# Layer 1's feed-forward: seven block products of sums in place of eight, a pair of batches at a time

## The chip, the cores and the metric

The kernel runs on one core of a Trainium2 chip. A core has five engines that run at the same time and meet at semaphores: TensorE (PE, matrix products; it loads a 128x128 operand, the weights, and streams the other through it), VectorE (DVE), ScalarE (ACT), GpSimd (POOL) and SyncE (SP, which here only issues DMAs). Each engine executes its own instructions in a fixed order. Operands lie in SBUF, 128 partitions wide; products land in PSUM, eight banks of 128 x 512 f32, which DVE and ACT can read and POOL can't. The metric is the time of one execution on the device in microseconds (us).

## The reference

Two layers, each with a cross attention and a feed-forward, over 4 batches of 512 tokens with 512 numbers each. The change touches the feed-forward of the last layer:

```python
up_gate = jnp.einsum('bsd,hd->bsh', x, W1)        # W1, W3: (2048, 512)
up_lin = jnp.einsum('bsd,hd->bsh', x, W3)
hidden = jax.nn.silu(up_gate) * up_lin
hidden = fwht(hidden)                             # Walsh-Hadamard over the 2048
out = jnp.einsum('bsh,dh->bsd', hidden, W2)       # W2: (512, 2048)
...
x = x + jnp.tanh(g_ffn[1]) * _L1_ffn_ref(_layernorm(x, axis=-1), ...)
```

## The kernel before

The order of the run is layer 0 (its attention and feed-forward), layer 1's attention, layer 1's feed-forward. Only the last part, and the pieces that are prepared for it during the attention, are touched.

*Number format.* PE takes f32 operands as they are for transposes, and a rounded form of them (fp32r) for most products. To keep the precision, an operand is split into a high part (rounded copy, made by ACT) and a low part (operand minus high, made by DVE from PSUM with `split`, by POOL from SBUF with `split_sb`). A product then takes three matmuls (`three`): high times low, low times high, high times high.

*Layer 1's feed-forward before* (L1391 to L1459). The 2048 hidden numbers are 16 tiles `f` of 128. For each tile the weights are prepared once (`prepare`): the rows of W1, W3 and of W2 (already partly transformed over the hidden index, from device memory) are loaded, transposed on PE against the identity into PSUM (`pw`), and split; W2's also go through a product with the 128x128 Hadamard matrix (`had`): transposes `pw`, a split into `hs`, the product `ph`, a split into `w2T`. The transforms of the hidden vector are so moved into W2. The normalised tokens of a batch are kept transposed and split (`xg`, by `normalise`).

The loop goes over pairs of tiles `n` (8 of them), in each over the 4 batches `b`, in each over the two tiles. Per tile and batch there is a product with W1 and one with W3: 4 chunks of the 512 input numbers x 3 matmuls, each 128x128 against 128x512, into a PSUM bank `p`. ACT takes the silu of the first (L1443), DVE multiplies by the second (L1444), `split_sb` makes high and low part `gg` on ACT and POOL (L125, L126), and `down` adds the product with W2 to four accumulators `acc` (L1419). After two tiles DVE adds the scaled `acc` to the residual `x` (L1454). In the last pair the result goes out by DMA.

*What sets the order.* The program is written in the order of the text, and the builder then orders each engine's instructions by its own simulated timeline. Where the text says `tc.manual_schedule(engines={nc.tensor.engine})`, PE keeps the order of the text. Before, that holds for layer 1's attention and not for the feed-forward. Side work (weights to prepare, tokens to normalise) is kept in a list `jobs` of generators; each call of `work()` takes the next steps up to a `yield`. A tile in SBUF or PSUM is reused by its tag in rotation (`bufs` of them), and its next writer waits for its last reader. All DMAs are issued by SP, in one order.

Of the kernel before, what the change touches and what calls it, by code (L numbers as in the profile page):

```python
# [21 lines left out]
P = 128  # L22
NB = 4
# [19 lines left out]
def flamingo_kernel(  # L43
# [52 lines left out]
    one_d = scratch("one_d", [2, S])  # L96

# [941 lines left out]
    with ExitStack() as l1:  # L1039
# [18 lines left out]
        def prepare(f, sp, bank, hp, htag, staged=None):  # L1058

            weights[f] = []
            fetched = []
            if staged is None:
                fetched.extend(fetch(f, i, sp) for i in range(2))
                yield
                yield
            pool, tag = (qz, f"qw{f % 2}") if f % 4 < 2 else (fi, f"w13_{f % 2}")
            w13 = pool.tile([P, 2, 2, ND, P], FR, tag=tag, name=f"w13T_{f}")  # L1070
            pairs = [w13[:, 0], w13[:, 1]]

            def kept(i, shape):
                wt = pairs[i] if i < 2 else w2_tile(f, f"w2T_{f}")
                weights[f].append((wt[:, 0], wt[:, 1]))
                return weights[f][-1]

            for i in range(3):
                st = fetched[i] if staged is None else staged[i]
                pt = bank([P, ND, P], f"pw{i}_{f}")  # L1080
                for k in range(ND):
                    nc.tensor.transpose(pt[:, k, :], st[:, k, :], ident)  # L1082
                if staged is None and i == 0:
                    fetched.append(fetch(f, 2, sp))
                if i < 2:
                    split(*kept(i, [ND, P]), pt)
                    yield
                    if staged is None and i:
                        yield
                        yield  # L1090
                        yield
            pt = pt.rearrange("p c q -> p (c q)")
            hs = [hp.tile([P, D], FR, tag=htag, name=f"hs{i}_{f}") for i in range(2)]
            split(*hs, pt)
            yield
            if staged is None:
                yield
            ph = bank([P, D], f"ph2_{f}")
            products(ph, [(had, hs[1]), (had, hs[0])])
            split(*kept(2, [D]), ph, 1.0 / math.sqrt(F))  # L1100
            yield

        xgT = [None] * NB

        def normalise(b, xg, xn_pool, bank, xn_tag="xn", ahead=False):

            xgT[b] = (xg[:, 0], xg[:, 1])
            return layernorm_split(b, f"g{b}", xg, xn_pool, bank, xn_tag, ahead)


        with ExitStack() as at:
# [216 lines left out]
            with tc.manual_schedule(engines={nc.tensor.engine}):  # L1328
                for s in range(-3, 4 * last + 2):
# [3 lines left out]
                    if s in (24, 40):  # L1333
                        jobs.append(prepare(s // 20 - 1, ap_, side, xnp, "xn"))
# [39 lines left out]
                    if s == 55:  # L1374
                        jobs.append(normalise(0, stack_tile(2, "xg0"), xnp, side, ahead=True))
                    if s > 20 and s % 16 == 6:
                        jobs.append(finish(n // NO - 1))
                    if s == 60:
                        jobs.append(normalise(1, stack_tile(0, "xg1"), xnp, side, ahead=True))
                    if s == 63:  # L1380
                        jobs.append(normalise(2, stack_tile(1, "xg2"), xnp, side, ahead=True))
# [9 lines left out]
        with ExitStack() as l2:  # L1391
            fi = pool_in(l2, "fi")
            fs = pool_in(l2, "fs", 3)
            gp = pool_in(l2, "gp1", 2)
            ps = pool_in(l2, "ps1", 3, space=PSUM)
            ps_acc = pool_in(l2, "ps_acc1", space=PSUM)
            side = banks_of(pool_in(l2, "ps_m1", 1, space=PSUM))

            def fetched(f):
                staged = [fetch(f, i, fs, 3) for i in range(3)]  # L1400
                jobs.append(prepare(f, fs, side, fs, "hs", staged))

            for n in range(NF // 2):
                for b in range(NB):
                    if n == 0 and b == 2:
                        xg3 = qz.tile([P, 2, ND, S], FR, tag="xn3", name="xg3")
                        jobs.append(normalise(3, xg3, fs, lambda shape, name: ps.tile(shape, F32, tag="h", name=name)))
                    if b < 2 and n + 1 < NF // 2:
                        fetched(2 * n + 2 + b)
                    acc = [  # L1410
                        ps_acc.tile([P, D], F32, tag=f"acc{t}", name=f"acc1_{n}_{b}_{t}")
                        for t in range(NT)
                    ]

                    def down(f, gs):
                        w = weights[f][2]
                        for t in range(NT):
                            for i, (a, c) in enumerate(three([g[:, ts(t, P)] for g in gs], w)):
                                nc.tensor.matmul(  # L1419
                                    acc[t], a, c,  # L1420
                                    start=(f % 2 == 0 and i == 0), stop=(f % 2 == 1 and i == 2),
                                )

                    pend = None
                    for f in (2 * n, 2 * n + 1):
# [21 lines left out]
                        if pend is not None:  # L1447
                            down(*pend)
# [45 lines left out]
```

## Time and profile before

| | us |
|---|---|
| median of 3 runs | 1350.21 (1341.34 to 1351.35) |
| the profiled execution | 1348.66 |
| its span in the profile | 1346.9 |

| engine | busy us of the span | instructions |
|---|---|---|
| PE | 1245.8 (92%) | 6217 |
| DVE | 679.1 (50%) | 1480 |
| ACT | 476.2 (35%) | 887 |
| POOL | 229.9 (17%) | 376 |

The profile is one execution recorded by the hardware. Its page cuts the span into 40 equal slices (33.7 us each) and gives for each the busy share in tenths, the clock that was granted to PE (`PEclk`, tenths of full speed), and the use of the DMA engines. Another view gives the same for any stretch of time: length, then for each engine busy time and number of instructions, the granted clock, the DMA engines' share and GB/s. A timeline lists instructions in order of time: start, duration, engine, line, operation, output and inputs, with the idle time before it and who ended it in brackets. The table of groups gives, behind the number of instructions, their busy time and the mean duration of one in ns, then the engine's idle time before them. A matmul's duration contains its pipeline: a 128x512 one lasts 394 ns, and the next starts earlier than that. Lines such as L131 are those of the kernel before; a helper's line stands for all who call it, so tiles' names tell more.

The stretch of 530 to 780 us, which is nearly all of layer 1's attention after its start, has PE busy for 216.32 us of 250 at a mean clock of 0.92, ACT for 123.41.

### The profile page before, as it was taken

The numbers are of one execution on the slowest core, as the hardware profiler recorded it, in microseconds if no ns is written. First come the engines' busy times: TensorE is split into PE (matmuls) and PEld (weight loads), VectorE is DVE, ScalarE is ACT, GpSimd is POOL, SyncE is SP. The second block draws the span as 40 slices with busy tenths as digits, with TensorE's granted clock in tenths as the row PEclk, the third lists the DMA queues.
The fourth block names the chain that finished last, engine by engine and source line by source line (L and its number), as shares of the span: only waits on it lengthen the run. The fifth ranks groups of instructions, "written<-read, shape, count | busy, mean of one in ns | idle before, by whom it ended". The sixth has DMA issues, their size and how long they took to land.

```text
span 1346.9 us, 16820 instructions
## 1 busy us (share of the span) xinstructions
PE 1245.8 (92%) x6217; PEld 938.2 (70%) x6217; DVE 679.1 (50%) x1480; ACT 476.2 (35%) x887; POOL 229.9 (17%) x376
## 2 busy tenths in 40 slices
PE   5999889999997779898989699999999999999998
PEld 4545677776784646464646488888888888888887
DVE  5976969698846454455654344233323232323222
ACT  4569633333432544445454612221212121212111
POOL 1000020000000224434444311111111111111111
PEclk9999899999997789898999899999999999999999
DMA  9791363615241545344340011000001010100002
GB/s 196 280 269 55 100 142 63 188 47 187 87 134 47 168 139 155 97 113 131 96 117 17 7 40 32 24 24 20 28 17 32 16 32 8 33 16 16 0 32 94
DMA packets 100011, 111.08 MB, mean 82 GB/s; under 512 B 12156, under 2 KB 64508, under 8 KB 98906
## 3 DMA queue, kind: packets, MB, share of 16 engines
q1 hardware_dynamic: 97570, 109.73, 28.9%
q8 instruction: 49, 0.80, 0.3%
q10 hardware_dynamic: 2360, 0.28, 0.2%
q14 instruction: 32, 0.26, 0.1%
HBM read 71.57 MB, written 38.15 MB: 81 GB/s over the span
## 4 chain that ended last, share of the span: by engine, by line
PE 68%; DMA 13%; DVE 8%; ACT 4%; SPq 3%; issue 2%; POOL 1%; DVEq 0%; ACTq 0%; POOLq 0%
PE p L131 26%; PE acc L1419 13%; PE pu L131 4%; PE acc L590 4%; PE pq L136 4%; PE pp L136 3%; DMA stk<-k_d 2%; PE sT L1166 2%; PE pav L1198 2%; PE sc L406 2%; PE den L1206 2%; PE pw L1082 1%; DMA qw<-in_L_ffn_up_kernel_dram 1%; DMA dn_q<-qw_d 1%; DVE x L626 1%
## 5 line engine op out<-in xcount | busy, mean ns | idle before, releaser
L131 PE MATMUL p<-xg,w13T 128*128 128x512 f32 x1536 | 382.7, 395 | 0.0
L131 PEld LDWEIGHTS p<-xg,w13T 128*128 128x128 f32 x1536 | 286.9, 188 | 65.0
L1419 PE MATMUL acc<-w2T,gg 128*128 128x512 f32 x768 | 199.0, 394 | 0.0
L126 POOL TENSOR_TENSOR gg<-s,gg 128x512 fp32r<-128x512 f32 x64 | 82.3, 1286 | 481.2 <-ACT gg L125 481.2
L1419 PEld LDWEIGHTS acc<-w2T,gg 128*128 128x128 f32 x768 | 142.4, 188 | 30.4
L1454 DVE SCALAR_TENSOR_TENSOR x<-acc,tg,x 128x512 f32<-128x512 f32 x128 | 87.8, 744 | 144.8 <-PE acc L1419 144.7
L131 PE MATMUL pu<-xnT,up_q 128*128 128x512 f32 x512 | 133.2, 403 | 3.7 <-ACT xT L791 1.8
L1170 ACT ACTIVATE e<-sT 128x384 f32<-128x384 f32 (+1 forms) x192 | 95.6, 529 | 73.5 <-PE sT L1166 72.2
L131 PEld LDWEIGHTS pu<-xnT,up_q 128*128 128x128 f32 x512 | 97.7, 193 | 28.4 <-ACT xT L791 2.3
L590 PE MATMUL acc<-dn_q,glo 128*128 128x512 f32 x256 | 102.2, 399 | 6.9 <-DVE glo L613 6.6
L125 ACT CAST gg<-s 128x512 fp32r<-128x512 f32 x64 | 39.7, 620 | 194.7 <-DVE s L1444 194.7
L1444 DVE TENSOR_TENSOR s<-s,p 128x512 f32<-128x512 f32 x64 | 43.9, 687 | 124.2 <-PE p L131 124.2
L590 PE MATMUL acc<-dn_q,ghi 128*128 128x512 f32 x256 | 100.9, 394 | 0.0
L419 DVE CUSTOM_DVE_ANT_0 junk<-sc,mask 128x384 f32<-128x384 f32 (+1 forms) x128 | 79.3, 619 | 42.6 <-PE sc L406 35.6
L1176 POOL TENSOR_SCALAR_AFFINE_SELECT e<-e 128x128 f32<-128x128 f32 (+1 forms) x192 | 62.9, 330 | 195.9 <-ACT e L1170 192.0
L406 PE MATMUL sc<-stk 96*128 96x128 f32 (+3 forms) x256 | 79.8, 359 | 16.2 <-DMA stk<-k_d 8.7
L1443 ACT ACTIVATE s<-p 128x512 f32<-128x512 f32 x64 | 38.2, 597 | 146.1 <-PE p L131 119.2
L609 ACT ACTIVATE ghi<-pu,up_b 128x512 fp32r<-128x512 f32 x64 | 44.1, 689 | 124.5 <-PE acc L590 116.4
L1166 PE MATMUL sT<-stk 98*128 98x512 f32 (+3 forms) x256 | 78.8, 361 | 7.3 <-DMA stk<-mr 4.1
L1166 PEld LDWEIGHTS sT<-stk 98*128 98x128 f32 x256 | 46.4, 197 | 37.6 <-issue 14.6
L415 DVE TENSOR_REDUCE fin<-sc 128x2 f32<-128x512 f32 (+1 forms) x48 | 32.3, 688 | 70.3 <-PE sc L411 70.3
L406 PEld LDWEIGHTS sc<-stk 96*128 96x128 f32 x256 | 46.8, 198 | 28.8 <-DVE fin L419 9.4
(231 smaller groups left out, 1638.2 us busy)
## 6 DMA issues: line engine op xcount, KB each, us to landing
qw_d<-qw SPq DMA_DIRECT2D x64, 128.0 KB
st<-in_L_ffn_W_dram SPq DMA_DIRECT2D x32, 256.0 KB
q_d<-qq SPq DMA_DIRECT2D x15, 512.0 KB
stk<-k_d SPq DMA_DIRECT2D x29, 256.0 KB
stk<-q_d SPq DMA_DIRECT2D x29, 256.0 KB
qw<-in_L_ffn_up_kernel_dram SPq DMA_DIRECT2D x32, 128.0 KB
qw<-n_L_ffn_down_kernel_dram SPq DMA_DIRECT2D x32, 128.0 KB
v_d<-vv SPq DMA_DIRECT2D x16, 256.0 KB
```

The source lines that it names most:

```text
L126: nc.gpsimd.tensor_sub(lo, src, f32(hi))
L131: nc.tensor.matmul(out, a, b, start=(i == 0), stop=(i == len(terms) - 1))
L136: nc.tensor.matmul(out, a, b, start=(i == 0), stop=(i == len(terms) - 1))
L406: nc.tensor.matmul(sc[:, g, :], qst[:96, g0 + g, ts(i, P)], kst[:96, g0 + g, :w], start=(g == 0 or not masked), stop=not masked,)
L419: nc.vector.tensor_tensor_reduce(junk[:, :w], sc[:, g, :], mask[:, S - w :], 1.0, -3.0e38, ALU.add, ALU.max, fin[:, i, g0 + g : g0 + g + 1],)
L590: nc.tensor.matmul(acc[t], g[:, ts(t, P)], dn[:, f % 4, :], start=(f == chunks[0] and i == 0), stop=(f == chunks[-1] and i == 1 and groups ...
L609: nc.scalar.activation(ghi, ph, AF.Gelu_apprx_tanh, bias=up_b[:, f : f + 1])
L1166: nc.tensor.matmul(sc[:, at_ : at_ + S - j * P], kst[:98, g, ts(j, P)], qst[:98, g, j * P :], start=True, stop=True,)
L1170: nc.scalar.activation(e[:, ds(EOFF[js[0]], w)], sc, AF.Exp)
L1176: nc.gpsimd.affine_select(diag, diag, [[0, len(js)], [1, P]], ALU.is_ge, 0.0, base=0, channel_multiplier=-1,)
L1419: nc.tensor.matmul(acc[t], a, c, start=(f % 2 == 0 and i == 0), stop=(f % 2 == 1 and i == 2),)
L1454: nc.vector.scalar_tensor_tensor(x[b][:, t, :], acc[t], tg[:, 3:4], x[b][:, t, :], ALU.mult, ALU.add)
```

## The change

The products of a pair of weight tiles (256 rows of W1 or W3) with a pair of batches are done as one block product of 2 x 2 blocks. With A the weights (A11, A12, A21, A22: first or second tile, first or second half of the 512 inputs) and B the tokens (B11 to B22: half of the inputs, batch of the pair), sums are formed first:

S1 = A21 + A22, S2 = S1 - A11, S3 = A11 - A21, S4 = A12 - S2; T1 = B12 - B11, T2 = B22 - T1, T3 = B22 - B12, T4 = B21 - T2.

Seven products of half the depth (2 chunks x 3 matmuls) replace eight: A11 B11, S2 T2, S1 T1, A12 B21, S3 T3, S4 B22, A22 T4, in this order (`chain`). Sums of them (p1, u, v on ACT and DVE) give the four results: for tile and batch (0, 0) behind A12, (1, 1) behind S3, (0, 1) behind S4, (1, 0) behind A22. 

The loop now has 16 blocks `n`: 8 pairs of tiles for batches 0 and 1, then the same 8 for batches 2 and 3. Each block has a chain with W1 (its results go through silu), then a chain with W3 (its results are multiplied in, `gate`, on POOL, in the last block of each pass on DVE). `down` for batch 1 (or 3) of the block before stands behind the fourth product of the first chain, for batch 0 (or 2) behind the second product of the second chain. In the first pass the weights are prepared for the next block and stored to device memory (`pack_d`, `w2T_d`); in the second they are loaded from there. `combine` makes the token sums from the residual, four tiles per pair of batches; the second pair's during block 7, the last block of the first pass. During the attention, W1 and W2 of the first two tiles are prepared (before: W1, W2, W3) and three of the four token tiles of the first pair (before: the normalised tokens of three batches). The whole loop stands under `manual_schedule` for PE. The core of the diff:

```diff
+    pack_d = [[scratch(f"pack_d{i}_{j}", [P, n * 4 * P]) for j, n in ((0, 4), (1, 3))] for i in range(NF)]
+    w2T_d = [scratch(f"w2T_d{f}", [P, 2 * D]) for f in range(NF)]
...
-        def prepare(f, sp, bank, hp, htag, staged=None):
...
+        def prepare13(n, i, rows, keep, bank, hp, htag, again=lambda: None):
+            m = 2 * n + i
+            sums, parts = pack(m)
+            pt = bank([P, 2, 2, P], f"pw{i}_{n}_0")
+            for k in range(ND):
+                nc.tensor.transpose(pt[:, k // 2, k % 2], rows[0][:, k, :], ident)
+            nc.scalar.copy(parts[:, :2, 0], pt)
+            first = keep()
+            nc.scalar.copy(first, pt)
+            nc.vector.tensor_sub(parts[:, :2, 1], pt, f32(parts[:, :2, 0]))
+            yield
+            pt = bank([P, 2, 2, P], f"pw{i}_{n}_1")
+            for k in range(ND):
+                nc.tensor.transpose(pt[:, k // 2, k % 2], rows[1][:, k, :], ident)
+            again()
...
+            nc.scalar.copy(s12[:, 0], pt[:, 0])
+            nc.vector.tensor_sub(s34[:, 0], first[:, 0], pt[:, 0])
+            nc.vector.tensor_add(s12[:, 0], s12[:, 0], pt[:, 1])
+            split(parts[:, 2, 0], parts[:, 2, 1], pt[:, 1])
+            nc.vector.tensor_sub(s12[:, 1], s12[:, 0], first[:, 0])
+            nc.vector.tensor_sub(s34[:, 1], first[:, 1], s12[:, 1])
+            yield
+            for j, t in enumerate((s12, s34)):
+                split_sb(sums[:, ts(j, 2), 0], sums[:, ts(j, 2), 1], t)
+            for j, t in enumerate((sums, parts)):
+                nc.sync.dma_start(pack_d[m][j], f32(t).rearrange("p s i c q -> p (s i c q)"))
+            yield
+
+        def prepare2(f, st, bank, hp, htag, again=lambda: None):
+            pt = bank([P, ND, P], f"pw2_{f}")
...
             hs = [hp.tile([P, D], FR, tag=htag, name=f"hs{i}_{f}") for i in range(2)]
             split(*hs, pt)
             yield
-            if staged is None:
-                yield
             ph = bank([P, D], f"ph2_{f}")
             products(ph, [(had, hs[1]), (had, hs[0])])
-            split(*kept(2, [D]), ph, 1.0 / math.sqrt(F))
+            weights[f] = wt = w2_tile(f, f"w2T_{f}")
+            split(wt[:, 0], wt[:, 1], ph, 1.0 / math.sqrt(F))
+            nc.sync.dma_start(w2T_d[f], f32(wt).rearrange("p i d -> p (i d)"))
             yield
...
+        def combine(pair, kind, room, bank, rooms, scalar=True):
+            names = (("B11", "T2"), ("T1", "B21"), ("T3", "B22"), ("T4",))[kind]
+            dst = room([P, len(names), 2, 2, S], f"tok{pair}_{kind}")
...
+                if scalar:
+                    nc.scalar.activation(o, y, AF.Identity, bias=nmr, scale=rstd)
+                else:
+                    nc.vector.tensor_scalar(o, y, rstd, nmr, ALU.mult, ALU.add)
+                return r
...
+                    pt = bank([P, 2, 2, P], f"pt_k{pair}_{kind}_{t}")
+                    for q, r in enumerate(ahead.pop(0)):
+                        for c in range(2):
+                            nc.tensor.transpose(pt[:, q, c], r[:, ts(c, P)], ident)
+                    split(dst[:, :, 0, :, ts(t, P)], dst[:, :, 1, :, ts(t, P)], pt)
+                    yield
...
-            ps = pool_in(l2, "ps1", 3, space=PSUM)
-            ps_acc = pool_in(l2, "ps_acc1", space=PSUM)
-            side = banks_of(pool_in(l2, "ps_m1", 1, space=PSUM))
+            ps = pool_in(l2, "ps1", 4, space=PSUM)
+            ps_acc = pool_in(l2, "ps_acc1", 2, space=PSUM)
+            side = banks_of(pool_in(l2, "ps_m1", 2, space=PSUM))
...
+            def chain(m, toks, name, take):
+                left = packs[m]
+                def product(a, b):
+                    h = ps.tile([P, S], F32, tag="h", name=f"p{a}_{name}")
...
+                h = product("A11", "B11")
+                p1 = room("p1")
+                nc.scalar.copy(p1, h)
+                yield
+                h = product("S2", "T2")
+                u = room("u")
+                nc.vector.tensor_add(u, p1, h)
+                yield
+                h = product("S1", "T1")
+                v = room("v")
+                nc.vector.tensor_add(v, u, h)
+                yield
+                h = product("A12", "B21")
+                take(0, 0, p1, h)
+                yield
+                h = product("S3", "T3")
+                nc.vector.tensor_add(u, u, h)
+                take(1, 1, v, h, qz.tile([P, S], F32, tag="qcols", name=f"c_{name}"))
+                yield
+                h = product("S4", "B22")
+                take(0, 1, v, h)
+                yield
+                h = product("A22", "T4")
+                take(1, 0, u, h)
+                yield
...
+            with tc.manual_schedule(engines={nc.tensor.engine}):
+                for n in range(2 * NN):
...
+                    def silu(q, j, a, b, room=None):
+                        acts[q, j] = s = gp.tile([P, S], F32, tag="s", name=f"s{n}_{q}_{j}")
+                        nc.vector.tensor_add(s, a, b)
+                        nc.scalar.activation(s, s, AF.Silu)
+
+                    def gate(q, j, a, b, room=None):
+                        s = acts[q, j]
+                        room = a if room is None else room
+                        nc.vector.tensor_add(room, a, b)
+                        (nc.vector if n % NN == NN - 1 else nc.gpsimd).tensor_mul(s, s, room)
+                        gs[q, j] = g = gp.tile([P, 2, S], FR, tag="gg", name=f"gg{n}_{q}_{j}")
+                        split_sb(g[:, 0], g[:, 1], s)
...
+                    for k, _ in enumerate(chain(2 * n, toks, f"1_{n}", silu)):
+                        work(2 if n == 0 else 1)
+                        if k == 3 and block:
+                            run(down(block, 1))
...
+                    for k, _ in enumerate(chain(2 * n + 1, toks, f"3_{n}", gate)):
+                        if k == 1:
+                            if block:
+                                run(down(block, 0))
+                            if first and n + 1 < NN:
+                                jobs.append(next2(n + 1))
+                            elif n + 1 < 2 * NN:
+                                load_w2(n + 1)
+                        if ends and k in (1, 3, 5):
+                            kind = k // 2
+                            jobs.append(
+                                combine(1, kind, pair_tile(kind), side, [(xnp, "xn", 2), (fs, "st", 6)], kind != 1)
+                            )
+                        work(2 if ends or n == 0 else 1)
```

`next13(n + 1, i)` and `next2(n + 1)` are `prepare13` and `prepare2` for the next block; `load_pack` loads a chain's stored blocks once the chain before the last has gone, `load_w2` the stored W2 tiles. A new `down` takes, per batch and 128 tokens, six matmuls (two tiles x three) into one of two banks `acc`, and DVE adds the bank to `x` (L1641 of the changed kernel).

## The prediction

> **What bounds the kernel now.** I read the strip of slices first (the last lines are the DMA engines and their GB/s), then the stage by stretches.
>
> ```profile
> PE   5999889999997779898989699999999999999998
> DVE  5976969698846454455654344233323232323222
> PEclk9999899999997789898999899999999999999999
> DMA  9791363615241545344340011000001010100002
> GB/s 196 280 269 55 100 142 63 188 47 187 87 134 47 168 139 155 97 113 131 96 117 17 7 40 32 24 24 20 28 17 32 16 32 8 33 16 16 0 32 94
> ```
> ```profile
> 900.00:1000.00 100.00, 100.00 (x451) 81.62 (x450) 29.06 (x44) 19.89 (x33) 15.43 (x12) 1.00 0.07 19
> ```
> The stage that changes, layer 1's feed-forward, is 772.2 to 1342.4 us (first `p` product, end of the last `acc`). TensorE (PE) is never idle there, at full clock; VectorE (DVE) works 29 us of 100, GpSimd (POOL) 15, DMA next to nothing. So a product less is time less, as long as PE stays fed. The timeline shows how it is fed:
>
> ```profile
> 1010.20 0.60 PE L1082 MATMUL pw<-ident,st 128*128 128x128 f32 x4
> 1010.84 0.59 ACT L117 CAST hs<-pw 128x512 fp32r<-128x512 f32 x1 [1.34 <-PE pw L1082]
> 1011.46 0.69 DVE L118 TENSOR_TENSOR hs<-pw,hs 128x512 fp32r<-128x512 f32 x1 [2.61 <-ACT hs L117]
> ...
> 1016.66 0.62 PE L131 MATMUL ph<-hs,had 128*128 128x512 f32 x2
> ...
> 1025.96 2.90 PE L1419 MATMUL acc<-w2T,gg 128*128 128x512 f32 x12
> ```
> The W2 transposes `pw` end, ScalarE (ACT) and DVE split them by 1012.2, and `ph`, which needs the split, is ordered 4.5 us later: the wait is filled with other products. Twelve `acc` take 2.74 us to the next group (1028.70): 0.228 each; 27 `p` from 1017.58 to 1023.89 give 0.234. I take 0.23. Four transposes take 0.35 (the next group starts 1010.55): 0.088 each. From PE's free moment to the consumer: 1010.55 to 1010.84; `ph` gives 0.20; I take 0.25.
>
> **Part by part.** Other prices:
>
> ```profile
> L1454 DVE SCALAR_TENSOR_TENSOR x<-acc,tg,x 128x512 f32<-128x512 f32 x128 | 87.8, 744 | 144.8 <-PE acc L1419 144.7
> L1444 DVE TENSOR_TENSOR s<-s,p 128x512 f32<-128x512 f32 x64 | 43.9, 687 | 124.2 <-PE p L131 124.2
> L419 DVE CUSTOM_DVE_ANT_0 junk<-sc,mask 128x384 f32<-128x384 f32 x64 | 35.3, 552 | 15.6 <-PE sc L406 13.0
> L241 DVE TENSOR_SCALAR xn_g<-x,rs_g,nmr_g 128x512 f32<-128x512 f32 x4 | 2.9, 755 | 0.0
> L126 POOL TENSOR_TENSOR gg<-s,gg 128x512 fp32r<-128x512 f32 x64 | 82.3, 1286 | 481.2 <-ACT gg L125 481.2
> L239 ACT ACTIVATE xn_g<-x,nmr_g,rs_g 128x512 f32<-128x512 f32 x12 | 10.1, 843 | 0.7 <-PE ph L131 0.7
> ```
> *Removed.* Per weight matrix, two hidden tiles and two batches, 48 matmuls become 7 x 6 = 42: 1536 to 1344, 192 x 0.23 = -44.2 us. *Added on PE:* the stage's transposes go from 168 + 16 (weights, last batch) to 176 + 64: 56 x 0.088 = +4.9. At the end four additions (2.73 together) followed the last product, now one: -0.5. Net -39.8.
>
> *The new waits.* The stage's PE order is now written by hand, so what PE waits for is not filled. The built program gives each engine's order. Products last 6 x 0.23 = 1.38.
>
> (a) Blocks 1 to 6, W2. PE's order is A12, `pw`, S3, `ph`; DVE's is: u and c of S3, and only then the low half of `hs`. With A12's end as zero, S3 ends at 1.73, u and c run 1.98 to 3.36, `hs` to 4.05; `ph` waits 2.35, and S4 and all later products queue behind it. The second tile's `hs` cast sits on ACT behind the cast of a gate product that POOL makes after three other operations (1.0 + 4 x 1.286 = 6.1; casts 0.62 and 0.59, DVE 0.69: 8.1), while PE reaches its `ph` at 7.7: 0.4 to 0.9. Sum 3.0 x 6 = 18.
>
> (b) Block 0 prepares twice as much (block 1's W1 and W3 beside its W2), and `ph` comes directly behind `pw`. After A12, DVE first adds its output and finishes W3's sums (0.69 + 4 x 0.42), ACT casts two of them (2 x 0.6), and only then `hs` is split (0.59 + 0.69): 0.25 + 2.4 + 1.2 + 1.3 = 5.1, against 0.35 of `pw` on PE: 4.8. For the second tile `w2T` (0.25 + 0.6 + 0.69), then u, c and `hs` on DVE (2.1) are 3.7 against 1.73 of PE: 2. Sum 7 (4 if DVE has the sums done early, 10 if the W3 load is late).
>
> (c) Block 7 builds the second pair's seven token blocks. From the last addition of block 6's output to the last transpose, DVE's list holds 24 operations of 0.69, 12 of 0.755, 24 of half width (0.42: 0.552 and 0.686 for 384 and 512 columns, one step further) and 4 of 0.744: 38.7. Queued operations overlap a little (four additions take 2.73, not 2.98): 35.6. PE has there 56 transposes, 30 products and 24 of the output: 4.9 + 6.9 + 5.5 = 17.3, and each transpose waits for its rows. Wait: 35.6 + 1 - 17.3 = 19 (12 if half-width ones cost 0.2; 22 without overlap).
>
> (d) Blocks 8 to 14: four gates cost POOL eight operations, not four. Their order puts batch 1's low half last but one: first multiply at 1.0 after A12, a gap of 0.7 behind c, then six of 1.255 (5.02 for four in a row at 771): 10.5; the output's second matmul comes up at 7 x 1.38 + 0.23 = 9.9. 0.7 x 7 = 5 (0 to 9, by 1.286 or by 1.1). No row shows POOL with a busier DVE beside it.
>
> (e) Block 15 has nothing behind which to hide: DVE multiply 1.5 after the last product, cast 0.65, POOL 1.3: 3.
>
> (f) End of attention: the first three token tiles need 12 full rows on ACT, as before, and 8 half rows more (0.5 each, an estimate from 0.843): 4 us, and 16 half-width sums on DVE (6.7). ACT is busy 18.2 of the 20 us from 740 to 760, and PE waits for it and for DVE there four times (1.25, 0.48, 0.81, 0.70): +2 (0 to 4). The 8 us hole at 760.8 to 768.9, PE waiting for a chain of DMAs, stays; the fourth tile's sums on DVE lie inside it.
>
> *Costed at nothing.* DVE's adds: 14 x 0.69 + 8 x 0.744 = 15.6 per block of 132 x 0.23 = 30.4, under PE whose four product banks let it run three products ahead; without that cover the 14 adds alone cost 9.7 a block. DMA: a block's weights are 2 x 1.84 + 1.05 = 4.7 MB, 155 GB/s, stored in the first half, loaded in the second; the strip moved 196 to 280. Each pack is issued on SP one and a half blocks ahead of its use, in the first half with stores in front of it that wait for POOL's casts; the raw rows behind those stores are needed a block later. If only 131 GB/s came (slice 19), a block would take 36: 5.5 x 16 = 88 is the upper end; I take 0, as the nearest row (long rows, slices 2 and 3) has 270.
>
> Sum: -39.8 + 18 + 7 + 19 + 5 + 3 + 2 = +14.
>
> *The clock.* A gap is followed by half clock here:
>
> ```profile
> 410.70 0.69 PE L406 MATMUL sc<-stk 96*128 96x384 f32 x1 [2.02 <-DVE fin L419]
> ```
> ```profile
> 406.00:409.00 3.00, 2.28 (x13) 1.30 (x11) 3.00 (x9) 0.59 (x1) 1.58 (x7) 1.00 0.00 0
> 409.00:412.00 3.00, 0.70 (x2) 0.33 (x2) 3.00 (x8) 0.00 (x0) 0.00 (x0) 0.61 0.00 0
> 412.00:415.00 3.00, 1.19 (x5) 0.79 (x5) 3.00 (x12) 1.28 (x2) 0.00 (x0) 0.50 0.00 0
> ```
> After 2.02 us idle the granted clock is 0.5; after 1.25 (at 740.9) it stayed 1.0. The waits of (a), (b), (e) are 2.35 and more, and in (c) PE is half idle. At 698 to 704 us three windows of 2 us give 0.95, 0.50 and 0.70: a short half-clock spell of some 3.4 us, worth 1.7 on a full PE. Ten would be 17; some falls into waits that are there anyway: +7 (0 to 20). Total +21.
>
> The Trainium skill ("TensorE: Matmul & The Clock Gate", "Why this matters for your kernels") asks for no idle gaps above about 3 us; by that none of the 2.35 us waits lowers the clock, and the sum would stay at +14. The 2.02 row speaks against it.
>
> **The rivals.** The profiled execution took 1348.66 (span 1346.9), 1.5 under the median; so about 1370.
> - *Forecast (0.55):* as summed, 1370 (1356 to 1388).
> - *Block 7 stays covered (0.22), not slower:* if DVE's list of (c) runs within PE's work, 19 and some 3 of the clock's share go: 1348 (1337 to 1357). It decides from 20 us for the list instead of 35.6. For: DVE is at 2 to 3 tenths in this stage today. Against: the list comes after block 6's last output in DVE's order, so none of it can be early, and its prices are rows of DVE itself.
> - *Only the product count matters (0.13):* PE stays at 10 tenths: 1349 - 40 = 1309 (to 1336). For: the stage's present rows. Against: `ph`.
> - *Transfers (0.10):* the pack loads come late: 1390 to 1440. Against: the strip.
>
> The change does do what it says: the built order has seven groups of six.
>
> **How the numbers follow.** 1% (13.5 us) is about what can be told from none. Faster: the third, and little of the second: 0.15. Same: most of the second, the low edge of the first: 0.24. Slower: 0.61. Range: 1337 (leaves out most of the third) to 1392 (leaves out most of the fourth). The forecast's own: 1356 to 1388.
>
> **What would show it.** Right: `ph` with some 2 us of idle behind DVE `hs` six times; a stretch of some 40 us before the second pair in which DVE is full and PE half; POOL `gg` ending a gap before `acc` in each late block; half clock there. Wrong: `ph` without idle, PE at 10 tenths through the first half, or DMA ending PE's waits.

## The result, and the profile after

The changed kernel takes 1397.23 us (median of 4 runs, 1396.03 to 1400.64) beside 1349.51 of the kernel before (1341.34 to 1351.35): a ratio of 1.037, 95% interval 1.0323 to 1.0416. The forecast was 1370 with a range of 1337 to 1392: the right side, but 21 of the 47 us, and the time lies 5 us above the range. The profiled execution took 1396.03, span 1394.3.

The strip of slices on the page of the changed kernel:

```profile
PE   5989899999986887988988679999988889999997
DVE  4977979697763544554644555665566765455545
PEclk9999999999987999999988899999999999999998
DMA  9791545434234454363410164344443343443321
```

In the kernel before, PE was at 9 from slice 24 to the last but one. Now it is at 7 in slice 24 and at 8 from slice 30 to 33; VectorE (DVE) has gone from 2 to 4 tenths to 4 to 7 in the second half, the DMA engines from next to none to mostly 3 or 4. Nothing here looks like 47 us: waits of a few us, and the clock behind them, vanish in slices of 35 us and tenths.

To see where the time went I took the stretches between landmarks. The start of a block is told from ScalarE's (ACT) copy of its first product A11. "Counted work" is products x 0.233 plus transposes x 0.088, the paces of the prediction; the excess is what is over. The excess of the first row is over the kernel before, which has the same attention there, with other side work. PE's idle time and the granted clock are from the view by stretches; the clock column sums (1 - clock) over windows of 4 us, and as part of such a window can be idle anyway, it is an upper bound. That of the first row leaves out the hole ahead of `rep`.

| stretch of the changed kernel | us | counted work | excess | PE idle | clock, at most | predicted |
|---|---|---|---|---|---|---|
| attention's end, last full `pp` group to `rep` (before: 32.7) | 41.8 | | 9.1 | 15.9 (before: 11.7) | 5.1 | (f) 2 |
| block 0 | 48.6 | 34.7 | 13.9 | 9.2 | 3.8 | (b) 7 |
| blocks 1 to 6 | 240.3 | 202.9 | 37.4 | 21.6 | 13.7 | (a) 18 |
| block 7 | 62.4 | 46.9 | 15.5 | 10.5 | 3.4 | (c) 19 |
| blocks 8 to 14 and half of 15 | 222.9 | 219.5 | 3.4 | 3.2 | 0 | (d) 5 |
| the end | 35.7 | 25.2, and 4.0 for the output | 6.5 | 3.9 | 4.2 | (e) 3 |

The excess adds up to 86; with 192 products less (-44.7 at 0.233), 56 transposes more (+4.9) and one addition instead of four at the end (-0.5) that is +46 of the 47.4 us by which the span grew. The prediction's terms add up to 61, with 7 for the clock in one sum. So nearly all of the loss is placed, and by place what the prediction lacks is 19 us in blocks 1 to 6, 7 in block 0 and 7 at the attention's end, less those 7; the other rows are off by 2 to 4 us, which cancel to 2.

The timeline around `ph` in block 1, the lines of four engines put together from four answers, in the order of time:

```profile
856.12 0.60 PE L1102 MATMUL pw<-ident,st 128*128 128x128 f32 x4
856.47 1.64 PE L135 MATMUL pS<-tok,pack 128*128 128x512 f32 x6
857.95 1.56 PE L135 MATMUL pA<-tok,pack 128*128 128x512 f32 x6
859.23 1.29 POOL L130 TENSOR_TENSOR pack<-sum,pack 128x512 fp32r<-128x512 f32 x1 [18.23 <-ACT pack L129]
859.35 0.60 PE L1124 MATMUL pw<-ident,st 128*128 128x128 f32 x4
859.71 1.65 PE L135 MATMUL pS<-tok,pack 128*128 128x512 f32 x6
861.36 0.58 ACT L121 CAST hs<-pw 128x512 fp32r<-128x512 f32 x1
861.48 1.27 POOL L1677 TENSOR_TENSOR s<-s,p 128x512 f32<-128x512 f32 x1 [0.96 <-DVE p L1676]
862.70 1.27 POOL L130 TENSOR_TENSOR pack<-sum,pack 128x512 fp32r<-128x512 f32 x1
864.00 0.69 DVE L122 TENSOR_TENSOR hs<-pw,hs 128x512 fp32r<-128x512 f32 x1 [1.32 <-POOL pack L130]
864.84 1.19 PE L135 MATMUL ph<-hs,had 128*128 128x512 f32 x2 [3.48 <-DVE hs L122]
```

PE's bracket names DVE's `hs`, as predicted. But DVE's own bracket names GpSimd's (POOL) `pack`: DVE stood idle for 1.32 us until POOL had read the sum of W1 or W3, at 862.70 to 863.97. `hs` is written into the buffer in which that sum lay: the tag `xn` has two buffers, and the two sums and the two halves of `hs` take turns in them. And POOL is late because a gate product (861.48) is ahead of the `pack`.

What follows such a wait, by stretches of 2 us:

```profile
862.00:864.00 2.00, 0.00 (x0) 0.00 (x0) 0.68 (x2) 0.62 (x1) 2.00 (x3) 0.93 0.63 177
864.00:866.00 2.00, 1.16 (x3) 1.00 (x4) 0.69 (x1) 0.00 (x0) 2.00 (x2) 0.50 0.62 262
866.00:868.00 2.00, 2.00 (x7) 1.52 (x6) 0.69 (x1) 1.10 (x2) 1.18 (x2) 0.50 0.68 274
868.00:870.00 2.00, 2.00 (x8) 1.70 (x7) 0.69 (x1) 0.52 (x1) 1.14 (x2) 0.50 0.65 258
870.00:872.00 2.00, 2.00 (x9) 1.55 (x9) 1.26 (x2) 0.18 (x2) 0.67 (x1) 0.86 0.37 109
```

The clock is at half for about 7 us, and PE is full again from 864.84. Each of blocks 1 to 6 has such a wait once and half clock behind it.

The attention's end, PE's waits in the timeline of the changed kernel and the clock there; the last two lines are the kernel before:

```profile
741.14 0.44 PE L1209 MATMUL pt_k<-ident,row 128*128 128x128 f32 x2 [1.37 <-DVE tok L122]
742.15 0.41 PE L1209 MATMUL pt_k<-ident,row 128*128 128x128 f32 x2 [0.57 <-DVE rs_g L212]
743.12 0.44 PE L1209 MATMUL pt_k<-ident,row 128*128 128x128 f32 x2 [0.39 <-DVE tok L122]
744.18 0.61 PE L1209 MATMUL pt_k<-ident,row 128*128 128x128 f32 x2 [0.62 <-DVE rs_g L211]
```
```profile
743.00:745.00 2.00, 1.25 (x5) 0.97 (x6) 1.90 (x10) 2.00 (x6) 0.29 (x1) 0.81 0.00 0
745.00:747.00 2.00, 2.00 (x12) 1.05 (x14) 0.97 (x3) 2.00 (x6) 1.13 (x2) 0.50 0.04 8
```
```profile
740.91 0.63 PE L255 MATMUL pt_g<-ident,xn_g 128*128 128x128 f32 x4 [1.25 <-ACT e L1170]
742.43 0.63 PE L255 MATMUL pt_g<-ident,xn_g 128*128 128x128 f32 x4 [0.48 <-DVE rs_g L208]
```

Here the token tiles' transposes wait in PE's fixed order, 2.95 us in four pieces. No piece is as long as the 2.02 us of the prediction's row, and still the clock falls. It falls once more behind waits of 1.74 and 0.52 (753.8 to 757.3), for 7 us, in which a wait of 0.59 lies. The kernel before waited 1.25, 0.48, 0.81 and 0.70 in the same part and stayed at 1.00.

### The profile page after: what moved, and what is told of

Its sections match the earlier page's. It is cut to its first block, busy times and chain, and to the rows that moved or that the text cites. A ratio compares the mean times of both kernels' runs of the same rounds, so it can differ in the third digit from the quotient of the medians.

```text
span 1394.3 us, 17517 instructions
## 1 busy us (share of the span) xinstructions
PE 1238.7 (89%) x6073; PEld 918.8 (66%) x6073; DVE 859.2 (62%) x1792; ACT 546.8 (39%) x1023; POOL 341.4 (24%) x464
## 4 chain that ended last, share of the span: by engine, by line
PE 58%; DVE 15%; DMA 10%; POOL 6%; ACT 5%; issue 4%; SPq 2%; DVEq 0%; ACTq 0%; POOLq 0%
PE acc L135 12%; PE pS L135 10%; PE pA L135 7%; PE acc L594 4%; PE pu L135 4%; PE pq L140 4%; PE pp L140 3%; PE pav L1318 2%; POOL s L1677 2%; PE sT L1286 2%; PE sc L410 2%; PE den L1326 2%; POOL gg L130 2%; DMA dn_q<-qw_d 1%; DVE x L630 1%
## 5 line engine op out<-in xcount | busy, mean ns | idle before, releaser
L135 PE MATMUL pS<-tok,pack 128*128 128x512 f32 x768 | 205.9, 411 | 0.0
L135 PE MATMUL acc<-w2T,gg 128*128 128x512 f32 x768 | 187.7, 398 | 7.5 <-POOL gg L130 3.9
L135 PEld LDWEIGHTS acc<-w2T,gg 128*128 128x128 f32 x768 | 145.8, 191 | 43.0 <-POOL gg L130 7.7
L135 PEld LDWEIGHTS pS<-tok,pack 128*128 128x128 f32 x768 | 147.2, 195 | 33.7
L135 PE MATMUL pA<-tok,pack 128*128 128x512 f32 x576 | 149.5, 402 | 0.0
L1641 DVE SCALAR_TENSOR_TENSOR x<-acc,tg,x 128x512 f32<-128x512 f32 x128 | 96.0, 751 | 82.5 <-PE acc L135 82.4
L135 PEld LDWEIGHTS pA<-tok,pack 128*128 128x128 f32 x576 | 109.7, 192 | 25.7
L1671 ACT ACTIVATE s<-s 128x512 f32<-128x512 f32 x64 | 40.4, 633 | 136.4 <-DVE s L1670 136.2
L130 POOL TENSOR_TENSOR pack<-sum,pack 128x512 fp32r<-128x512 f32 x32 | 40.8, 1285 | 149.2 <-ACT pack L129 149.2
```

The source lines that it names most:

```text
L130: nc.gpsimd.tensor_sub(lo, src, f32(hi))
L135: nc.tensor.matmul(out, a, b, start=(i == 0), stop=(i == len(terms) - 1))
L1641: nc.vector.scalar_tensor_tensor(x[b][:, t, :], acc, tg[:, 3:4], x[b][:, t, :], ALU.mult, ALU.add)
L1671: nc.scalar.activation(s, s, AF.Silu)
```

## The experiments

Each is one edit of the changed kernel, but for the last four versions. Their times are medians beside the 1397.23 above; the kernel before had 1347 to 1351 in the same sessions. The part ahead of the attention's last full `pp` group, which no edit touches, took 732 to 746 us in the profiles of these kernels, so a few us of a median can come from there: the length of the stretch that was edited says more.

**Room for `hs`.**

```diff
+            hsp = pool_in(l2, "hsp", 2)
-                        2 * n + j, raw[n, 2][j], side, xnp, "xn",
+                        2 * n + j, raw[n, 2][j], side, hsp, "hs",
```

> Only edit to the changed kernel: the two split halves hs of a W2 tile get two buffers of their own in the stage, instead of taking turns with the sums of W1 and W3 in one tag of two buffers. Theory A (the buffer sets the wait: in the changed kernel's trace VectorE's hs of 864.00 is ended by GpSimd's pack, 1.32 us, and GpSimd has a gate product in front of that): the wait before ph in blocks 1 to 6 falls from 3.48 us to 1 or less, the half-clock spells behind it go with it, a block goes from 39.3-40.6 us to 35-36, block 0 loses some 4 us; in all -28 to -36 us: 1361 to 1369. Theory B (the prediction's: VectorE's own order, u and c ahead of hs): 2.35 us of wait stay, -7 us in all, half clock stays: 1390.

1363.5 us (1359.21 to 1371.51): -34. PE and DVE in block 1 of this kernel:

```profile
850.22 0.68 DVE L122 TENSOR_TENSOR hs<-pw,hs 128x512 fp32r<-128x512 f32 x1
850.82 0.67 DVE L1617 TENSOR_TENSOR u<-u,pS 128x512 f32<-128x512 f32 x1
851.41 0.68 DVE L1677 TENSOR_TENSOR c<-v,pS 128x512 f32<-128x512 f32 x1
850.95 0.73 PE L135 MATMUL ph<-hs,had 128*128 128x512 f32 x2 [0.69 <-DVE hs L122]
```

The wait is 0.69, the clock 1.00 in blocks 1 to 6; blocks 1 to 5 take 35.3 to 35.4 us instead of 39.3 to 40.6, and block 0's wait of 6.78 became 1.40 (48.6 to 42.1 us). DVE now has `hs` ahead of u and c: nothing but the buffer was edited, so the order that the prediction took for the cause came with the buffer. What u and c in front would cost with the buffer free was not run. Theory A holds.

**The wait filled.** 36 transposes of no use in front of the first `ph`:

```diff
             ph = bank([P, D], f"ph2_{f}")
+            for k in range(36 if f % 2 == 0 and f > 2 else 0):
+                nc.tensor.transpose(ph[:, ts(k % ND, P)], ident, ident)
```

> Only edit to the changed kernel: in blocks 1 to 6, TensorE makes 36 more 128x128 transposes of the identity (36 x 0.088 = 3.2 us) into the bank of ph ahead of the first ph, so that the wait of 3.48 us is filled with work of no use. Theory A (half clock follows TensorE's idle gap): the wait stays as long, but the clock stays 1.00 in those blocks; the 20 us windows from 840 to 1080 lost 14 us to it, so -10 to -14 us: 1383 to 1387. Theory B (the half clock comes from something else in these stretches, as the transfers or the weight loads): no gain, 1396 to 1400. If the transposes are late, at most +0.5 us a block.

1389.22 us (1381.76 to 1394.92): -8, between the two theories (10 to 14, or nothing). One stretch of 160 us of both kernels, of the changed one and then of this:

```profile
840.00:1000.00 160.00, 146.07 (x643) 117.72 (x643) 94.70 (x153) 56.42 (x104) 61.19 (x49) 0.94 0.43 159
```
```profile
840.00:1000.00 160.00, 157.41 (x805) 130.40 (x804) 95.60 (x156) 56.86 (x106) 62.89 (x50) 1.00 0.46 167
```

The transfers run on as before, DVE's `hs` stands behind POOL as long (1.36 us), PE only doesn't rest: and the clock is 1.00. So the half clock follows PE's own pause. Blocks 1 to 6 took 234.6 us instead of 240.3; as the fill delays `ph` by some 0.4 a block, I estimate the clock's cost there at 8 us. The 13.7 of the table is too much: part of each spell lies inside the wait, and PE at full clock comes early to the second tile's `ph` and waits 0.65 there, which it didn't in the changed kernel.

**Rows of the first pair on DVE**, in the attention:

```diff
-                            combine(0, kind, pair_tile(kind), side, [(xnp, "xn", 2), (ap_, "st", 2)])
+                            combine(0, kind, pair_tile(kind), side, [(xnp, "xn", 2), (ap_, "st", 2)], False)
```

> Only edit to the changed kernel: the rows of the first pair's token tiles that are made during the attention are scaled by VectorE instead of ScalarE. Theory A (the 9.1 us that the attention's end lost, from the last full pp group to rep, come from 8 half rows of 0.61 us and 12 full ones on a ScalarE that also makes the exponentials): that stretch falls from 41.8 us towards the 32.7 of before, by 5 to 9 us: 1388 to 1392. Theory B (VectorE, with its splits and half-width sums, is as late, or the reciprocal of the denominators waits longer behind it): within 3 us of 1397, or slower.

1396.44 us (1393.69 to 1402.05), no change that can be told. PE's waits there became fewer and longer:

```profile
748.27 0.41 PE L1209 MATMUL pt_k<-ident,row 128*128 128x128 f32 x2 [2.33 <-DVE tok L122]
749.85 0.44 PE L1209 MATMUL pt_k<-ident,row 128*128 128x128 f32 x2 [1.17 <-DVE row L1194]
761.57 0.63 PE L1209 MATMUL pt_k<-ident,row 128*128 128x128 f32 x4 [1.43 <-DVE row L1191]
```

The stretch to `rep` is 37.9 us in this profile against 41.8, less than theory A's 5 to 9, and the medians don't show it; by the time alone theory B holds. PE's waits there now name DVE's rows: what is taken from ACT is late on DVE.

**Two of the three tiles out of the attention**, one into the hole ahead of `rep`, one into block 0.

```diff
-                    if s in (55, 60, 63):
+                    if s in (55,):
...
+                for kind in (1,):
+                    for _ in combine(0, kind, pair_tile(kind), side, [(xnp, "xn", 2), (ap_, "st", 2)]):
+                        pass
             next(quotients)
...
+            for kind in (2,):
+                jobs.append(combine(0, kind, pair_tile(kind), side, late_rooms))
```

> Only edit to the changed kernel: two of the three token tiles of the first pair are no longer made among the attention's last units: one is made in the 10 us in which TensorE waits for the chain of transfers ahead of rep, the other at the start of block 0. Theory A (the side work of these tiles, in TensorE's fixed order, on ScalarE and VectorE together, costs the 7 us from the last full pp group to the end of the attention's products, half of it as half clock): that stretch goes from 31.6 us down by 4 to 7, the wait for rep stays at 9 to 11, block 0 pays 0 to 3: 1390 to 1395. Theory B (the stretch is longer for another reason): no change there, and block 0 pays 3 to 5: 1399 to 1402.

1403.5 us (1401.63 to 1408.25): 6 more. The stretch to `rep` went to 31.9, a little under the kernel before: the tiles are what lengthened it. The tile in the hole cost nothing:

```profile
771.48 2.02 PE L1209 MATMUL pt_k<-ident,row 128*128 128x128 f32 x8 [5.78 <-DVE row L1191]
773.88 2.07 PE L1374 MATMUL rep<-rows_d,spread 32*128 32x512 f32 x4 [0.39 <-DMA rows_d<-rden_d]
```

But block 0 took 56.3 instead of 48.6, and 2 us more lay between `rep` and its first copy: the tile moved into it, and half clock, took back what was won: within the profile the edit comes to nothing, and the other 6 us lie ahead of it, where nothing was edited. Theory A is right about the attention's end and wrong about the price in block 0.

**Block 7**, first the 28 sums of half rows on POOL:

```diff
-            add, sub = nc.vector.tensor_add, nc.vector.tensor_sub
+            sums = nc.gpsimd if pair else nc.vector
+            add, sub = sums.tensor_add, sums.tensor_sub
```

> Only edit to the changed kernel: the half-width sums of the second pair's rows (28 operations of 128x256) go to GpSimd instead of VectorE. Theory A (VectorE's list sets block 7: 32.9 us without a gap from 1095.4 to 1128.3): 28 x 0.34 = 9 us less on VectorE, block 7 falls from 62.4 us to 54-57: 1389 to 1392. Theory B (the sums are on the way of every transpose, and one on GpSimd is dearer): block 7 the same or longer, 1397 to 1405.

1391.55 us (1388.92 to 1398.47), theory A's time; block 7 went from 62.4 to 57.5. Then all scaling on ACT as well (`scalar` left at its default in both calls):

```diff
-                                combine(1, kind, pair_tile(kind), side, [(xnp, "xn", 2), (fs, "st", 6)], kind != 1)
+                                combine(1, kind, pair_tile(kind), side, [(xnp, "xn", 2), (fs, "st", 6)])
```

> Only edit to the changed kernel: for the second pair's rows the half-width sums go to GpSimd and all scaling to ScalarE, so that VectorE loses 28 sums of 0.34 us and 16 scalings of 0.46 and keeps some 18 us in block 7; GpSimd has 28 of 0.8 and four gate halves of 1.3 there, 27 us. Theory A (whichever engine's list is longest sets block 7): 62.4 us go to 54 to 56, one or two below the kernel with the sums alone on GpSimd (57.5): 1389 to 1391. Theory B (the chain ScalarE row, GpSimd sum, transposes, split, with two banks, sets it): 57 to 60.

1392.9 us (1389.25 to 1401.1), no gain over the edit before that the medians can tell; block 7 is 55.9, as theory A has it. The middle of the block in the changed kernel and in this one:

```profile
1100.00:1120.00 20.00, 12.33 (x58) 8.85 (x56) 20.00 (x37) 8.94 (x15) 5.09 (x4) 0.91 0.26 92
```
```profile
1100.00:1120.00 20.00, 14.13 (x69) 10.77 (x68) 14.10 (x21) 17.84 (x30) 19.00 (x22) 0.91 0.30 106
```

DVE was full to the last, 20.00 of 20; now POOL is (19.00) and PE still waits, for rows of POOL (1.29 and 2.40 us). Of the excess of 15.5 us 6.5 are gone and 9 stay, though DVE's busy time in the block fell by 14.7 us (48.8 to 34.2): another engine's list is next.

**The end**: the 24 products of block 14's second half behind the last product of block 15. (The edit also gives the last block's gates a free tile to write to.)

```diff
-                            if block:
+                            if block and n < 2 * NN - 1:
                                 run(down(block, 0))
...
+                    if n == 2 * NN - 1:
+                        run(down(block, 0))
```

> Only edit to the changed kernel: in the last block the output's second half of the block before (24 products, 5.6 us) stands behind the last product instead of behind the second, with a free tile as room for the gates' results. Theory A (the wait of 3.19 us for the last gate, 0.66 behind it and the half clock after them cost the end 4 to 6 us): the wait is filled, 1391 to 1394. Theory B (the end is set by the last transfer, or the wait moves on to the last gate of the other batch): within 2 us of 1397.

1395.43 us (1394.13 to 1400.29). The changed kernel's last products, and this kernel's:

```profile
1375.58 0.69 PE L135 MATMUL acc<-w2T,gg 128*128 128x512 f32 x1 [3.19 <-ACT gg L129]
1376.93 13.54 PE L135 MATMUL acc<-w2T,gg 128*128 128x512 f32 x47 [0.66 <-POOL gg L130]
```
```profile
1373.02 2.88 PE L135 MATMUL acc<-w2T,gg 128*128 128x512 f32 x12
1376.91 3.04 PE L135 MATMUL acc<-w2T,gg 128*128 128x512 f32 x12 [1.02 <-DVE x L1641]
```

The last stretch fell from 35.7 to 29.8 us, as theory A has it. The median fell by 2 only, which is theory B's figure: the part ahead of the stage, which is the same in both, varies by several us from run to run (first copy at 784.4 and 788.8 in these two profiles).

**The stores twice**: each pack goes out a second time, to memory that nobody reads.

```diff
                 nc.sync.dma_start(pack_d[m][j], f32(t).rearrange("p s i c q -> p (s i c q)"))
+                nc.sync.dma_start(pack_x[m][j], f32(t).rearrange("p s i c q -> p (s i c q)"))
```

> Only edit to the changed kernel: in the first pass every block pack of W1 and W3 is stored twice, the second time to device memory that nobody reads: 14 to 16 stores of 1.8 MB more, some 28 MB in 300 us, on top of 90 to 240 GB/s. Theory A (the transfers are hidden and no wait of TensorE in the stage ends with one): within 4 us of 1397. Theory B (stores hold back the raw rows or the pack buffers): some us for each of 7 blocks, 1410 or more.

1398.11 us (1394.59 to 1402.57). Of 800 to 1080, the changed kernel and this one:

```profile
800.00:1080.00 280.00, 249.55 (x1098) 199.47 (x1098) 168.83 (x284) 106.58 (x196) 109.61 (x86) 0.94 0.45 167
```
```profile
800.00:1080.00 280.00, 248.68 (x1106) 198.87 (x1105) 171.49 (x289) 107.73 (x197) 109.22 (x86) 0.95 0.68 266
```

266 GB/s instead of 167, and no difference: the transfers of the first pass are hidden. In the second, PE's only waits are those of 0.46 us for POOL.

**All together**: room for `hs`, both moves of tiles, block 7 and the end.

> All of it: buffers of its own for hs (-34 measured), and the three edits above. Theory A (the waits stand one behind another on TensorE, so that their prices add): -34 - 5 - 8 - 5 = -52: 1340 to 1350, near the kernel before. Theory B (a wait that is taken away is partly paid by the next one): 1350 to 1360.

1350.56 us (10 runs, 1346.72 to 1357.03); ratio to the kernel before 1.0009, 0.9985 to 1.0033. The median lies where the ranges of the two theories meet. By the stretches of the single runs (-32.0 for the room, in the stage; -6.5; -5.8; nothing for the tiles) some 1353 was due. So the waits add, as in theory A, but for the tiles, for which it had 5 us and which gave nothing.

Two versions followed, in which the two W2 tiles are transposed one behind the other ahead of both `ph` (the second tile's `hs` lie in `xn` again), and DVE makes one of the four gate products in the second pass. One has the third token tile in the hole, the other leaves it in the attention. The edits beyond the version before, of which the last is in `next2`:

```diff
-            sums = nc.gpsimd if pair else nc.vector
+            sums = nc.gpsimd if pair and kind in (0, 3) else nc.vector
...
-                        (nc.vector if n % NN == NN - 1 else nc.gpsimd).tensor_mul(s, s, room)
+                        (nc.vector if n % NN == NN - 1 or (not first and (q, j) == (0, 0)) else nc.gpsimd).tensor_mul(s, s, room)
...
+                for _ in range(2):
+                    for step in steps:
+                        next(step)
+                        yield
```

> The changed kernel with the edits that paid: room for hs, the late output half of the end, block 7's scaling on ScalarE (the sums of kinds 0 and 3 on GpSimd, of 1 and 2 on VectorE); and three new ones. Both W2 tiles are transposed before the first ph, so that each ph has at least one more product in front of it; in the second pass VectorE does one of the four gate products; of the attention's three token tiles only the third is moved, into the hole ahead of rep. Theory A (the waits add): from 1350.6, ph's 0.69 and 1.4 us go in all first blocks (-6), GpSimd's 0.46 goes in seven (-3), block 0 is at 42 us instead of 48.6 and the attention's end at 35-38 instead of 32 (-2), block 7 within 2 us of 56: 1337 to 1343. Theory B (what is taken away comes back as another wait): 1346 to 1354.

> The same without the move of the third token tile: the attention's end is that of the changed kernel (40 to 42 us from the last full pp group to rep). Theory A (the tile costs the attention's end its share where ScalarE is full): 2 to 5 us more than the run before. Theory B (the tile is no slower there than in the hole): the same within 1.5 us.

1345.98 us (0.998, 0.9952 to 1.0008) and 1348.76 (0.9993, 0.9963 to 1.0022): the first misses theory A's 1337 to 1343. Blocks 1 to 6 are 34.2 to 35.8 us without a wait for `hs`, blocks of the second pass 30.6 instead of 31.2. The attention's end didn't shorten (40.8 and 40.2); the medians differ by 3, within their intervals, and from the last full `pp` group on the two profiles take 604.5 and 603.8 us. So moving this tile gained nothing that shows. In block 0 the new order cost 2.7 (44.8 against the 42.1 with room for `hs` alone). So, last, with the second tile in the hole and block 7's sums all on POOL again:

```diff
-                    if s in (55, 60, 63):
+                    if s in (55, 63):
...
+                for _ in combine(0, 1, pair_tile(1), side, [(xnp, "xn", 2), (ap_, "st", 2)]):
+                    pass
...
+                for j in (0, 1, 0, 1) if n > 1 else (0, 0, 1, 1):
+                    next(steps[j])
+                    yield
```

> The kernel of 1346.0 with three places taken from what the runs so far showed: in the attention only the token tiles of kinds 0 and 2 are left, and that of kind 1 is made in the hole ahead of rep; block 0 prepares its W2 tiles one after the other again; block 7 has all its row sums on GpSimd. Theory A (the waits add, and an attention end with less side work is short whatever is taken out of it): attention's end, last full pp group to rep, 33 to 36 us instead of 40.8, block 0 at 42 instead of 44.8, block 7 at 56 instead of 58: 1334 to 1340. Theory B (the 9 us there come back as waits in the hole or in block 0, as they did when two tiles were moved): 1343 to 1348.

1334.55 us (8 runs, 1330.44 to 1344.02) beside 1346.94: a ratio of 0.9909, 0.9871 to 0.9947: some 1% under the kernel before, small but clear of the noise. The attention's end is 34.5, block 0 39.6, block 7 57.1, the end 29.8. PE's only waits at the hole:

```profile
772.74 2.15 PE L1210 MATMUL pt_k<-ident,row 128*128 128x128 f32 x8 [5.44 <-DVE rden L1360]
776.34 2.07 PE L1375 MATMUL rep<-rows_d,spread 32*128 32x512 f32 x4 [1.45 <-DMA rows_d<-rden_d]
```

## Why the prediction fell short

*In sum*, the waits were forecast and the clock was not. PE's idle time is 53 us (48.4 in the stage, 4.2 more than before at the attention's end) beside 54 for the terms (a) to (f). That these agree is in part luck: (c) was 8.5 us too much, (a), (b) and (f) too little, and the cause behind (a) and (b) was another. The other 33 us of the excess are time in which PE counts as busy, and for that the prediction had the clock's +7 and nothing else. There lie the 26 us that the forecast lacks: the step that failed is the clock's term, 7 where some 23 were lost.

*The products* were right: -44.7 at the measured pace, and in the second pass a block takes 31.2 us for 132 products, as counted, with 0.46 of wait.

*Step (a)* had the right place and waiter, but not the cause. "DVE's is: u and c of S3, and only then the low half of `hs`" was read from the built order; that the order came from a buffer that POOL still had to read was not asked. So 2.35 became 3.48, 21.6 for six blocks instead of 18, and 0 instead of 0.4 to 0.9 for the second tile. With room of its own the wait is 0.69: shown.

*Step (b)*, 7: measured 6.78 and 1.40 on `ph` and 9.2 idle in all. The size was near, but here too DVE stood idle in front of `hs` for POOL's `pack` (3.81 us, to 821.41); with room for `hs` the two waits are 1.40 and 1.55.

*Step (c)*, 19: DVE's list ran 32.9 us without a gap (predicted 35.6; a scaling took 0.535 on average, not 0.755), but PE was idle for 10.5 and the excess is 15.5. The mechanism held; the two edits of the block showed it, and that POOL comes next.

*Steps (d) and (e)*: 0.46 in seven blocks is 3.2 (5 predicted); 3.19 and 0.66 at the end are 3.9 (3 predicted).

*Step (f)*, "+2 (0 to 4)", failed: 9.1. Its waits were nearly right (5.8 us against 3.2 before). Two things were left out of it. PE's clock, for which the prediction doesn't name this stretch, having read that "after 1.25 (at 740.9) it stayed 1.0", fell twice, for a loss of up to 5.1 us in the part up to 768 (read from the rows; no run filled these waits). And "the fourth tile's sums on DVE lie inside" the hole, costed at nothing, stood in front of the reciprocal's second half: from the reciprocal (772.19) to the next DMA 2.7 us instead of 1.1; the hole is 10.07 instead of 8.13.

*The clock*, "+7 (0 to 20)", failed in size. By the granted clock up to 24 us more than before were lost from `rep` on and 5.1 in the attention's end, 29 together; with 8 us for blocks 1 to 6, as estimated from the run with the wait filled, in place of 13.7, some 23. The prediction counted ten spells worth 1.7 each and took 10 of these 17 us to fall into waits. From 741 us to the last product there are 12 beside that of the hole, 5 of them 6.8 us long, and most of each lies behind its wait, on a full PE. The Trainium skill ("TensorE: Matmul & The Clock Gate", "Why this matters for your kernels") asks for no idle gaps above about 3 us; by that there would have been none after the shorter waits. The rows at 741 to 745 speak against it as the row of 2.02 did.

*What no term held*: with the clock at 1.00 and the wait at 0.69, a first-pass block takes 35.3 us for 33.8 of counted work. A product behind a group of transposes takes 1.48 us instead of 1.40 (856.47 to 857.95, and 857.95 to 859.35 above), which a pace of 0.088 taken inside a group can't show. With six groups that is 0.5 of the 0.8 us that are left of a block, some 3 us in all. The 7 us or so between this, the clock's 23 and the 33 above aren't placed.

*The rivals.* Block 7 was not covered. The transfers cost nothing, shown with the stores doubled in the first pass and by PE's waits in the second. That only the product count matters is what the second pass looks like, and the first comes near with its wait gone (34.2 us for 33.8 of counted work in the last version): that one, at 1334.55, keeps 12 of the 40 us. Block 7 still has 10 us of excess there, block 0 5 and the attention's end 2 more than before; whether they can go was not tried.

## What to carry to other kernels

A count of products is worth its full price only on an engine that stays fed; once the order is fixed by hand, every wait is added to it, and then the clock's share of it. Here the waits came to 53 us and the clock to some 23 behind them. When an engine's order looks unlucky, ask what each instruction's output buffer waits for before blaming the order: a tag with two buffers shared by two chains tied TensorE to GpSimd here, and 4 KB a partition were worth 34 us. Side work that is moved needs a place where all engines that it uses are free: the hole in front of a transfer had it, the start of the next stage didn't.

## What the hardware showed beyond that

The granted clock doesn't ask for one long gap. Four waits of 1.37, 0.57, 0.39 and 0.62 us, with PE busy for 3.04 us of the 6 from 739 to 745, were followed by half clock; in the kernel before, waits of 1.25 and 0.48, with PE busy for 4.27 of the 6 us from 739 to 745, were not. Where between the two the border lies, these rows don't say. Filling a gap with work of no use kept the clock at 1.00 (the run with 36 transposes).

DVE operations that read only SBUF were stretched beside POOL. A half-row sum with both inputs in SBUF takes 0.42 us alone and 1.45 where it starts just behind a POOL operation of 1.29 in the changed kernel:

```profile
858.07 0.42 DVE L1111 TENSOR_TENSOR sum<-sum,first 128x256 f32<-128x256 f32 x1
859.35 1.45 DVE L1112 TENSOR_TENSOR sum<-first,sum 128x256 f32<-128x256 f32 x1
```

And the scaling of a row on DVE, 0.535 on average there, took 0.894 in the kernel with the sums on POOL (12 of them in each). The Trainium skill ("SBUF — State Buffer", "Who interferes with whom") says that a DVE instruction with two inputs in SBUF contends with a POOL instruction that reads SBUF, and that the ports they share are an exclusive lock. The 1.45 agrees: the sum ends at 860.80, 0.28 us behind the POOL operation of 859.23 to 860.52. In the prediction POOL and DVE were priced as if they were alone.
